# State-space scan and attention kernel: late bfloat16 splits, normalization on ScalarE, a third open convolution, first loads reordered

## The chip, the cores and the metric

The kernel runs on one core of one Trainium2 chip. The metric is device time in microseconds of one execution. Eight executions took 10527.92 to 10549.25 us, median 10539.07. The engines are TensorE (PE, its weight loads PEld), VectorE (DVE), ScalarE (ACT), GpSimd (POOL) and SyncE (SP), whose queue issues nearly all DMAs.

## What is computed

The input `x` is 8 images of 64 x 64 tokens of 96 channels. Layer 0 is a state-space block, layer 1 an attention without softmax and a feed-forward with 8-bit products:

```python
x = x + conv_ref(group_norm(x))                   # layer 0
t = tokens(x)
t = t + attn_ref(layer_norm(t))                   # layer 1
t = t + ffn_ref(layer_norm(t))
# conv_ref:
xin, z = split(einsum(x, in_proj_w))              # 192 channels each
xc = silu(depthwise_conv_3x3(xin) + conv_b)
xs = [row-wise, column-wise, and both reversed]   # K = 4 directions
dts, Bs, Cs = split(einsum(xs, x_proj_weight))    # 6, 16, 16 rows
delta = softplus(dts @ dt_projs_weight + bias)
h = h * exp(delta * A) + (delta * u) * B          # 4096 steps, 16 states
y = sum over n of h * C, + D * u                  # the four directions added
out = (layer_norm(y) * silu(z)) @ out_proj_w
```

## The kernel before

Three passes follow each other: `pass1` (L233), the projections and convolutions of all batches; `pass2` (L517), the scans; `pass3` (L823), everything after. Memory pools are opened per pass. What one pass hands to the next goes through DRAM.

**Order of work.** Each kind of work is a Python generator that names the engine and an assumed cost before each of its instructions, or a key that must be done. `weave` (L140) lets at most `room[kind]` units of a kind be open, and picks again and again the unit whose step can start earliest by these costs, the lower rank winning a tie. `InOrder` (L81) keeps the instructions of each engine in the order in which they were picked. So every engine, SP's queue too, works strictly in order, and a waiting instruction holds all behind it. The helper `issue` (L88, L89) records nearly all instructions, which is why the profile has L89 almost everywhere.

**Pass 1**, by pairs of batches. The 192 channels of two batches are cut in three chunks of 128: the first 128 channels of either batch, and the last 64 of both.
- `statistics` (L305) loads 512 tokens (`xs`), transposes them on PE into one of two PSUM buffers `pt`, and takes `bn_stats` on DVE. `group_norm` (L320) makes mean and inverse deviation `gm` of a batch; its power runs as two tiny POOL operations.
- `projection` (L348), eight units a batch, loads and transposes the tokens again (`xt`, `pt`), normalizes them to `xn` on DVE as (x - mean) times inverse deviation, multiplies by the weights on PE (`pa`, three products), and lets ACT copy to the padded image `xpad` and make SiLU of `z`. A batch's projections need the convolution that used its `xpad` before.
- `convolution` (L397) runs nine taps over 4096 elements on DVE into `u`, then SiLU and a transposed copy `ut` on ACT, and stores. Its taps wait for the taps of the convolution before it; the chunks go in the order 0, 2, 1.
- `x_projection` (L445), 16 units a batch, multiplies `u` on PE (`px`, three PSUM buffers) and copies the result to `xd` (ACT; every second one on DVE in the last batch; three buffers), which is stored to `xd_d`.
- `split` (L473), six units a batch, makes three bfloat16 parts of the rows for B and for delta, whose sum is the float32 value: it loads `bq` from `xd_d`; ACT casts it to part 0; a subtraction leaves the rest in `bq`; ACT casts part 1; a second subtraction gives part 2; two DMAs store `bs` to `b_d` or `dt_d`. The subtractions are POOL's, and DVE's in the last batch.

**Pass 2** takes 192 pieces: 4 pairs x 3 channel chunks x 4 directions x 4 pieces of 1024 steps; chunks 0 and 1 are full (one batch on 128 partitions), chunk 2 is split between two batches. `prepare` (L548) loads `xdt` (six DMAs), then `xb` and `u`, and makes B transposed (`bT`), `delta`, `du` = delta * u and its transpose `duT`. For each of 16 states n, `decay` (L619) makes `da` = exp(delta * A) on ACT, `products` (L657) brings du * B into a PSUM buffer `wide` (three of them) by one of three ways (`WAYS`: ACT's `x`, POOL's `xg`, or DVE's product), and `scan` (L681) runs the recurrence on DVE into `h`. For each two states, `load_c` (L607) loads C spread over the partitions (`c`, 1 MB, six buffers), `times_c` (L720) multiplies by `h` on POOL, and `sum_over_n` (L734) adds into `acc` on PE. The `xb` and `xdt` of a piece are the splits of its two batches; C is read from `xd_d` in float32.

**Pass 3** is not touched.

Of the kernel before, what the change touches and what calls it, by code (L numbers as in the profile page):

```python
# [33 lines left out]
F32 = mybir.dt.float32  # L34
# [8 lines left out]
P = 128  # L43
# [10 lines left out]

WAYS = [([2, 4, 6, 8, 10, 12, 14, 15], [3, 9]), ([3, 5, 7, 10, 13, 15], [2, 6, 12])]
NS = 3
GRP = 512
NG = L // GRP
RPG = GRP // WW
# [169 lines left out]
    return a_neg, dsum, dt_b, dt_w, sel, sel2  # L229


@with_exitstack
def pass1(ctx, tc, g, consts, ident, mhalf, engines, u_d, z_d, xd_d, b_d, dt_d):  # L233
    nc = tc.nc
# [85 lines left out]
    def group_norm(b):  # L320

        yield "st", b
        yield "dve", 0.2
        mv = two.tile([C, 2], F32, name="mv")
        dve.bn_aggr(mv, sts[b].rearrange("p a b -> p (a b)"))
        yield "pe", 0.3, 0.3, mms
        pm, slot = ps_mm.tile([P, GRP], F32, name="pm", tag="mm"), mms.taken
        pe.matmul(pm[0:C, 0:1], gmat, mv[:, 0:1], start=True, stop=True)
        end = yield "dve", 0.5
        mms.release(slot, end)  # L330
        gm = wp.tile([C, 2], F32, name=f"gm{b}")
        dve.tensor_copy(gm[:, 0:1], pm[0:C, 0:1])
        dq = two.tile([C, 1], F32, name="dq")
        dve.tensor_sub(dq, mv[:, 0:1], gm[:, 0:1])
        dve.scalar_tensor_tensor(dq, dq, dq, mv[:, 1:2], ALU.mult, ALU.add)
        yield "pe", 0.3, 0.3, mms
        pv, slot = ps_mm.tile([P, GRP], F32, name="pv", tag="mm"), mms.taken
        pe.matmul(pv[0:C, 0:1], gmat, dq, start=True, stop=True)
        end = yield "dve", 0.2
        mms.release(slot, end)  # L340
        dve.tensor_copy(gm[:, 1:2], pv[0:C, 0:1])
        end = yield "pool", 1.0
        pool.tensor_scalar(gm[:, 1:2], gm[:, 1:2], 1e-5, None, ALU.add)
        pool.tensor_tensor(gm[:, 1:2], gm[:, 1:2], mhalf[0:C, 0:1], ALU.pow)
        gms[b] = gm
        done["stats", b] = end

    def projection(b, q):  # L348

        pair, j = b // 2, b % 2  # L350
        cols = slice(q * GRP, (q + 1) * GRP)
        rows = slice(1 + q * RPG, 1 + (q + 1) * RPG)
        inner = slice(1, WW + 1)
        own, other = slice(64 * j, 64 * j + 64), slice(64 - 64 * j, P - 64 * j)
        third = xpad[2 + pair % 2]
        yield "stats", b
        yield "sp", 0.6, 4.0
        x = transposed(four, "xt", b, q)
        next(x)
        if pair > 0:  # L360
            yield "conv", pair - 1, j
        if pair > 1:
            yield "conv", pair - 2, 2
        yield "pe", 0.7, 0.3, pts
        pt, slot = next(x), pts.taken
        end = yield "dve", 0.8
        pts.release(slot, end)
        xn = four.tile([C, GRP], F32, name="xn")
        dve.tensor_scalar(xn, pt[0:C, :], gms[b][:, 0:1], gms[b][:, 1:2], ALU.subtract, ALU.mult)
        def product(w):  # L370
            yield "pe", 0.75, 0.4, mms
            p = ps_mm.tile([P, GRP], F32, name="pa", tag="mm")
            pe.matmul(p, w, xn, start=True, stop=True)
            return p, mms.taken

        pa, slot = yield from product(w_in[:, 0:P])
        end = yield "act", 0.6
        act.copy(xpad[j][:, rows, inner], pa.rearrange("p (h w) -> p h w", w=WW))
        mms.release(slot, end)
        pa, slot = yield from product(w_mix[:, j, :])  # L380
        yield "act", 0.6
        act.copy(third[own, rows, inner], pa[own, :].rearrange("p (h w) -> p h w", w=WW))
        z1 = three.tile([P, GRP], F32, name="z1")
        end = yield "act", 0.6
        act.activation(z1[other, :], pa[other, :], AF.Silu)
        one_more(("proj", b), NG, end)
        mms.release(slot, end)
        pa, slot = yield from product(w_in[:, DI : DI + P])
        z0 = three.tile([P, GRP], F32, name="z0")
        end = yield "act", 0.6  # L390
        act.activation(z0, pa, AF.Silu)
        mms.release(slot, end)
        yield "sp", 0.9
        sp.dma_start(z_d[b][P:DI, cols], z1[other, :])
        sp.dma_start(z_d[b][0:P, cols], z0)
# [49 lines left out]
    def x_projection(b, o, q):  # L445
        pair, j = b // 2, b % 2
        yield "u", pair, j
        yield "u", pair, 2
        px = None
        for ty, u in ((0, us[pair, j]), (1 + j, us[pair, 2])):  # L450
            end = yield ("pe", 0.62, 0.4) if px else ("pe", 0.62, 0.4, pxs)
            if px is None:
                px, slot = ps_px.tile([P, GRP], F32, name="px", tag="px"), pxs.taken
            if o == 0:
                src = u[:, q * GRP : (q + 1) * GRP]
            else:

                src = u.rearrange("p (h w) -> p h w", w=WW)[:, :, q * RPG : (q + 1) * RPG]
            pe.matmul(px, w_xp[:, ty, o, :], src, start=ty == 0, stop=ty > 0)
        one_more(("xproj", b), 2 * NG, end)  # L460
        by_dve = b == NB - 1 and q % 2 == 1
        end = yield ("dve" if by_dve else "act"), 0.6 if o == 0 else 0.8
        xd = three.tile([2 * NXD, GRP], F32, name="xd")
        src, dst = px[0 : 2 * NXD, :], xd
        if o == 1:
            src, dst = src.rearrange("p (h w) -> p w h", w=RPG), xd.rearrange("p (w h) -> p w h", w=RPG)
        (dve.tensor_copy if by_dve else act.copy)(dst, src)
        pxs.release(slot, end)
        end = yield "sp", 0.9, 3.0
        sp.dma_start(xd_d[b][o][:, q * GRP : (q + 1) * GRP], xd)  # L470
        one_more(("xd", b, o), NG, end)

    def split(b, o, row, rows, pieces, at, dst):  # L473

        wide, used = GRP, rows * pieces
        name, cost, by = ("dve", 0.65, dve) if b == NB - 1 else ("pool", 4.4 if b < NB - 2 else 2.5, pool)
        yield "xd", b, o
        yield "sp", 0.7, 4.0
        bq = three.tile([P, wide], F32, name="bq")
        src = xd_d[b][o][row : row + rows].rearrange("r (s t) -> (r s) t", s=pieces)  # L480
        sp.dma_start(bq[0:used], src[:, at : at + wide])
        yield "act", 0.6
        bs = three.tile([P, NS, wide], BF16, name="bs")
        act.copy(bs[0:used, 0, :], bq[0:used])
        yield name, cost
        by.tensor_sub(bq[0:used], bq[0:used], bs[0:used, 0, :])
        yield "act", 0.6
        act.copy(bs[0:used, 1, :], bq[0:used])
        yield name, cost
        by.tensor_sub(bs[0:used, 2, :], bq[0:used], bs[0:used, 1, :])  # L490
        yield "sp", 0.9
        half = used // 2
        for k2 in range(2):
            to = dst[k2].rearrange("e n (s t) -> (n s) e t", s=pieces)[:, :, at : at + wide]
            sp.dma_start(to, bs[half * k2 : half * (k2 + 1)])

    units = []
    for pair in range(NB // 2):
# [7 lines left out]
        for b in batches:  # L506
            for o in range(2):
                units += [("xproj", x_projection(b, o, q)) for q in range(NG)]
                units += [("split", split(b, o, 0, 2 * N, 4, at, b_d[b][o])) for at in (0, GRP)]
                units.append(("split", split(b, o, DT0, 2 * R, 8, 0, dt_d[b][o])))  # L510
    later_loads()
    room = {"proj": 4, "norm": 1, "stats": 3, "xproj": 3, "split": 3, "conv": 2}
    weave([(kind, (list(room).index(kind), i), unit) for i, (kind, unit) in enumerate(units)], room, done)


# [1 line left out]
def pass2(ctx, tc, g, ident, engines, fixed, u_d, xd_d, b_d, dt_d, y_d):  # L517
# [22 lines left out]
    def one_more(key, of, end):  # L540
        counts[key] = counts.get(key, 0) + 1
        if counts[key] == of:
            done[key] = end
# [4 lines left out]
    def prepare(at):  # L548
# [4 lines left out]
        parts = chunk_rows(pair, c)  # L553
        if at > 1:
            yield "scans", at - 2
        yield "sp", 2.5, 3.0
        xdt = one.tile([2 * NS * NS * R, T], BF16, name="xdt")
        for j in range(2):
            for m in range(NS):
                row = (j * NS + m) * NS * R  # L560
                sp.dma_start(xdt[row : row + NS * R, :], dt_d[2 * pair + j][o][k2].rearrange("s r t -> (s r) t")[:, cols])
        yield "sp", 1.5, 3.0
        xb = two.tile([KB, T], BF16, name="xb")
        for j in range(2):
            sp.dma_start(xb[j * NS * N : (j + 1) * NS * N, :], b_d[2 * pair + j][o][k2].rearrange("s n t -> (s n) t")[:, cols])
# [37 lines left out]
        act.copy(made[at][4], pt)  # L603
        slots["wide"].release(slot, end)
        done["duT", at] = end

    def load_c(at, m):  # L607
        pair, c, k, pc = pieces[at]
# [187 lines left out]
    for at, (pair, c, k, pc) in enumerate(pieces):  # L796
# [19 lines left out]
                add("term", 0, times_c(at, n // 2), n)  # L816
                add("sum", -4, sum_over_n(at, n // 2), n)
        add("acc", 0, take_acc(at), N)
    weave(units, {"prep": 1, "c": 1, "da": 2, "x": 1, "xg": 1, "dbu": 2, "scan": 2, "carry": 1, "term": 1, "sum": 1, "acc": 1}, done)


@with_exitstack
# [283 lines left out]
```

## Time and profile before

| what | value |
|---|---|
| median of 8 runs | 10539.07 us |
| profiled execution, its own time | 10533.8 us |
| its span | 10532.0 us |
| busy: DVE / ACT / POOL / PE | 9636.3 / 9296.5 / 9255.2 / 7582.7 us |
| mean granted TensorE clock | 0.901 |
| first tap of the first convolution | 72.6 us |
| end of the last tap of the last convolution | 701.3 us |
| first decay `da` of the scan pass | 807.3 us |

A line of a timeline gives start, duration, engine, line, operation, output and inputs, and in brackets how long the engine had been idle and what ended that. A line of a group gives the shape and the count, then busy time and mean nanoseconds of one, then the idle time just ahead of its instructions and what ended most of it. A line of the stage windows gives for each engine the busy time and the number of instructions, then the granted clock, the busy share of the DMA engines and what they moved. `SPq` is SP's queue. Neighbouring records of one engine overlap by some hundredths of a microsecond.

### The profile page before, as it was taken

The page shows a single profiled execution, that of the slowest core. Times are in us where ns is not written, and L with a number is a line of the kernel's source. Part 1 is how long each engine was busy: PE and PEld are TensorE (multiplying, and loading weights), DVE is VectorE, ACT ScalarE, POOL GpSimd, SP SyncE. Part 2 cuts the span into 40 slices and gives each one's busy share as a digit, 9 for nine tenths or more (in the row PEclk, how much of TensorE's full clock was granted, in tenths as well). Part 3 has the DMA queues.
Part 4 walks back from the last instruction along what each step waited for, and adds up shares of the span by engine and source line. Part 5 has one row for each costly group of instructions (what it writes and reads, how often), then busy time and mean ns, then how long its engine had stood idle before and what let it go on. Part 6 is the DMA issues. An engine that isn't in the chain of part 4 may idle for free.

```text
span 10532.0 us, 151336 instructions
## 1 busy us (share of the span) xinstructions
PE 7582.7 (72%) x51232; PEld 6175.8 (59%) x51232; DVE 9636.3 (91%) x6986; ACT 9296.5 (88%) x21363; POOL 9255.2 (88%) x3259
## 2 busy tenths in 40 slices
PE   6756777777677777777677777777777777776887
PEld 3325666566556566665565666655566666655665
DVE  7868999999999999999999999999999999997776
ACT  4649999999999999999999999999999999996665
POOL 2548999999999999999999999999999999997886
PEclk8878999998999999989999999988999999997776
DMA  5766666678976666699966666899766667997442
GB/s 155 231 199 201 203 221 212 218 206 199 203 216 209 217 218 209 214 200 200 215 209 217 214 213 214 202 202 200 218 210 216 218 203 217 201 200 177 123 130 60
DMA packets 928008, 2103.21 MB, mean 200 GB/s; under 512 B 274391, under 2 KB 422648, under 8 KB 925700
## 3 DMA queue, kind: packets, MB, share of 16 engines
q1 hardware_dynamic: 919812, 2092.79, 69.9%
q8 instruction: 410, 6.72, 0.3%
q14 instruction: 362, 2.97, 0.1%
q10 hardware_dynamic: 7424, 0.74, 0.1%
HBM read 1917.59 MB, written 175.66 MB: 199 GB/s over the span
## 4 chain that ended last, share of the span: by engine, by line
ACT 28%; DVE 22%; issue 17%; PE 16%; POOL 12%; DMA 4%; SPq 1%; DVEq 0%; POOLq 0%; ACTq 0%
DVE h L89 15%; ACT x L89 13%; ACT da L89 10%; POOL c L89 8%; PE wide L89 6%; PE acc L89 6%; DVE wide L89 4%; PE mm L89 2%; DMA xd_d<-xd 1%; ACT L89 1%; DVE u L89 1%; PE pa L89 1%; DMA xdt<-dt_d 1%; POOL xg L89 1%; ACT delta L89 1%
## 5 line engine op out<-in xcount | busy, mean ns | idle before, releaser
L89 POOL TENSOR_TENSOR c<-c,h 128x2048 f32<-128x2048 f32 x1536 | 6967.3, 4550 | 396.8 <-DVE h L89 336.4
L89 DVE TENSOR_TENSOR_SCAN h<-da,carry,wide 128x1024 f32<-128x1024 f32 x2304 | 5253.1, 2330 | 206.5 <-PE wide L89 137.7
L89 ACT ACTIVATE x<-duT,bT 128x128 f32<-128x128 f32 (+1 forms) x14336 | 4154.9, 366 | 57.1 <-PE wide L89 51.2
L89 PE MATMUL acc<-ident,c 128*128 128x128 f32 x24576 | 3472.1, 297 | 554.2 <-POOL c L89 546.0
L89 ACT ACTIVATE da<-delta,a_neg 128x1024 f32<-128x1024 f32 x3072 | 3504.0, 1144 | 346.4 <-DVE h L89 335.1
L89 PEld LDWEIGHTS acc<-ident,c 128*128 128x128 f32 x24576 | 3125.1, 155 | 886.8 <-POOL c L89 753.0
L89 PE MATMUL wide<-ident,x 128*128 128x128 f32 x11264 | 1605.5, 290 | 866.1 <-DVE h L89 845.0
L89 PEld LDWEIGHTS wide<-ident,x 128*128 128x128 f32 x11264 | 1336.5, 149 | 1162.1 <-DVE h L89 512.5
L89 DVE TENSOR_TENSOR_SCAN h<-da,wide 128x1024 f32<-128x1024 f32 x768 | 1707.7, 2270 | 84.9 <-PE wide L89 61.1
L89 DVE TENSOR_TENSOR wide<-du,wide 128x1024 f32<-128x1024 f32 x1216 | 1458.7, 1211 | 142.1 <-PE wide L89 141.9
L89 PE MATMUL wide<-xb,sel 96*128 96x512 bf16 x2432 | 751.8, 394 | 598.3 <-DVE h L89 505.8
L89 POOL TENSOR_TENSOR xg<-duT,bT 128x512 f32<-128x512 f32 (+1 forms) x640 | 892.3, 1410 | 78.0 <-PE wide L89 58.1
L89 PEld LDWEIGHTS <-sel 96*128 96x128 bf16 x2432 | 222.3, 101 | 789.0 <-DVE h L89 392.8
L89 PE MATMUL wide<-ident,xg 128*128 128x128 f32 x3584 | 498.4, 284 | 246.6 <-DVE h L89 240.2
L89 PEld LDWEIGHTS wide<-ident,xg 128*128 128x128 f32 x3584 | 410.0, 146 | 323.7 <-issue 155.9
L89 POOL TENSOR_TENSOR du<-delta,u 128x1024 f32<-128x1024 f32 x192 | 455.2, 2371 | 139.4 <-ACT delta L89 129.7
L89 ACT ACT_TABLE_LOAD x385 | 494.0, 1283 | 6.8
L89 DVE SCALAR_TENSOR_TENSOR u<-xpad,conv_w,u 128x4096 f32<-128x4096 f32 x96 | 452.7, 4716 | 1.2
L89 PE MATMUL px<-u,w_xp 128*128 128x512 f32 x512 | 260.0, 647 | 105.2 <-ACT u L89 65.1
L89 PE MATMUL mm<-w_out,gt 128*128 128x96 f32 (+1 forms) x1024 | 267.3, 381 | 40.2 <-POOL gt L89 21.8
L89 PEld LDWEIGHTS mm<-w_out,gt 128*128 128x128 f32 (+1 forms) x1024 | 204.2, 246 | 105.4 <-issue 36.3
L89 PE MATMUL wide<-ident,du 128*128 128x128 f32 x1536 | 210.4, 282 | 61.9 <-DVE h L89 44.5
(133 smaller groups left out, 5877.6 us busy)
## 6 DMA issues: line engine op xcount, KB each, us to landing
c<-xd_d SPq DMA_DIRECT2D x1024, 1024.0 KB
c<-xd_d SPq DMA_DIRECT2D x1024, 512.0 KB
u<-u_d SPq DMA_DIRECT2D x128, 512.0 KB
xdt<-dt_d SPq DMA_DIRECT2D x1152, 36.0 KB
xb<-b_d SPq DMA_DIRECT2D x384, 96.0 KB
u<-u_d SPq DMA_DIRECT2D x128, 256.0 KB
y_d<-y SPq DMA_DIRECT2D x24, 1024.0 KB
y<-y_d SPq DMA_DIRECT2D x64, 384.0 KB
```

What stands on the lines that cost most here:

```text
L89: ins = getattr(self.engine, op)(*args, **kwargs).ins
```

## The change

1. `split` leaves `pass1`, becomes a function of its own, and always subtracts on POOL, at an assumed cost of 4.4. Batches 0 to 4 are still split in pass 1, two splits open at a time instead of three. The 18 splits of batches 5, 6 and 7 (`LATE = 5`) are made in pass 2, one at a time, with buffers of their own; split i gets the rank of piece 5 (i + 1). `prepare` waits for the splits of its late batches.
2. `xn` is made by ACT as scale * x + bias straight from PSUM; `group_norm` gets one more small DVE operation, which waits for POOL's power, for the bias.
3. Three convolutions may be open instead of two, and four x-projections instead of three with four `xd` buffers instead of three.
4. In the first piece of pass 2, the loads of `xb` and `u` are picked together with those of `xdt`, so that fewer C loads stand ahead of them in SP's queue.

```diff
+LATE = 5
+def split(engines, pool_of, src, row, rows, pieces, at, dst):
+    act, pool, sp = engines
+    wide, used = GRP, rows * pieces
+    yield "sp", 0.7, 4.0
+    bq = pool_of.tile([P, wide], F32, name="bq")
+    src = src[row : row + rows].rearrange("r (s t) -> (r s) t", s=pieces)
+    sp.dma_start(bq[0:used], src[:, at : at + wide])
+    yield "act", 0.6
+    bs = pool_of.tile([P, NS, wide], BF16, name="bs")
+    act.copy(bs[0:used, 0, :], bq[0:used])
+    yield "pool", 4.4
+    pool.tensor_sub(bq[0:used], bq[0:used], bs[0:used, 0, :])
+    yield "act", 0.6
+    act.copy(bs[0:used, 1, :], bq[0:used])
+    yield "pool", 4.4
+    pool.tensor_sub(bs[0:used, 2, :], bq[0:used], bs[0:used, 1, :])
+    yield "sp", 0.9
+    half = used // 2
+    for k2 in range(2):
+        to = dst[k2].rearrange("e n (s t) -> (n s) e t", s=pieces)[:, :, at : at + wide]
+        sp.dma_start(to, bs[half * k2 : half * (k2 + 1)])
+def splits(b, o, b_d, dt_d):
+    return [(0, 2 * N, 4, at, b_d[b][o]) for at in (0, GRP)] + [(DT0, 2 * R, 8, 0, dt_d[b][o])]
...
-        end = yield "pool", 1.0
+        yield "pool", 1.0
         pool.tensor_scalar(gm[:, 1:2], gm[:, 1:2], 1e-5, None, ALU.add)
         pool.tensor_tensor(gm[:, 1:2], gm[:, 1:2], mhalf[0:C, 0:1], ALU.pow)
+        end = yield "dve", 0.2
+        dve.scalar_tensor_tensor(gm[:, 0:1], gm[:, 0:1], -1.0, gm[:, 1:2], ALU.mult, ALU.mult)
...
-        end = yield "dve", 0.8
+        end = yield "act", 0.6
         pts.release(slot, end)
         xn = four.tile([C, GRP], F32, name="xn")
-        dve.tensor_scalar(xn, pt[0:C, :], gms[b][:, 0:1], gms[b][:, 1:2], ALU.subtract, ALU.mult)
+        act.activation(xn, pt[0:C, :], AF.Identity, bias=gms[b][:, 0:1], scale=gms[b][:, 1:2])
...
-        xd = three.tile([2 * NXD, GRP], F32, name="xd")
+        xd = four.tile([2 * NXD, GRP], F32, name="xd")
...
-                units += [("split", split(b, o, 0, 2 * N, 4, at, b_d[b][o])) for at in (0, GRP)]
-                units.append(("split", split(b, o, DT0, 2 * R, 8, 0, dt_d[b][o])))
+                if b < LATE:
+                    units += [("split", after(("xd", b, o), split((act, pool, sp), two, xd_d[b][o], *w))) for w in splits(b, o, b_d, dt_d)]
-    room = {"proj": 4, "norm": 1, "stats": 3, "xproj": 3, "split": 3, "conv": 2}
+    room = {"proj": 4, "norm": 1, "stats": 3, "xproj": 4, "split": 2, "conv": 3}
...
+        for b in (2 * pair, 2 * pair + 1):
+            if b >= LATE:
+                yield "split", b
         yield "sp", 2.5, 3.0
         xdt = one.tile([2 * NS * NS * R, T], BF16, name="xdt")
...
-        yield "sp", 1.5, 3.0
+        if at > 0:
+            yield "sp", 1.5, 3.0
         xb = two.tile([KB, T], BF16, name="xb")
...
+    def late_split(b, o, which):
+        yield from split((act, pool, sp), one, xd_d[b][o], *which)
+        one_more(("split", b), 6, 0.0)
...
-    weave(units, {"prep": 1, "c": 1, "da": 2, "x": 1, "xg": 1, "dbu": 2, "scan": 2, "carry": 1, "term": 1, "sum": 1, "acc": 1}, done)
+    last = [(b, o, w) for b in range(LATE, NB) for o in range(2) for w in splits(b, o, b_d, dt_d)]
+    units += [("split", 5 * N * (i + 1), late_split(*which)) for i, which in enumerate(last)]
+    weave(units, {"prep": 1, "c": 1, "da": 2, "x": 1, "xg": 1, "dbu": 2, "scan": 2, "carry": 1, "term": 1, "sum": 1, "acc": 1, "split": 1}, done)
```

## The prediction

> **What bounds the kernel now.** I read the stage windows first. The scan pass runs from about 810 to 9600 us and is 83% of the span; the change touches the pass before it, the hand-over, and the first quarter of the scan pass.
>
> Windows of the convolution stretch (72 to 702), of the hand-over (702 to 812), and of two scan stretches (full and split channel chunks):
>
> ```profile
> core 0: us, PE busy (x) PEld busy (x) DVE busy (x) ACT busy (x) POOL busy (x), PEclk, DMA share, GB/s
> 72.00:702.00 630.00, 453.31 (x1230) 208.41 (x1228) 557.70 (x242) 353.79 (x477) 298.67 (x84) 0.86 0.67 203
> 702.00:812.00 110.00, 35.39 (x89) 15.40 (x90) 13.94 (x21) 39.60 (x50) 16.04 (x13) 0.66 0.66 210
> 860.00:1560.00 700.00, 505.08 (x3706) 429.44 (x3705) 670.19 (x349) 654.96 (x1427) 652.36 (x171) 0.93 0.65 212
> 2320.00:2980.00 660.00, 463.90 (x3251) 393.70 (x3249) 617.90 (x326) 641.57 (x1724) 617.30 (x208) 0.90 0.91 201
> ```
>
> DVE paces the convolutions (89% busy, 72.3 us idle). In the hand-over nothing is busy: a chain of waits. In the scans DVE leads (95.7%), with POOL (93.2%) and ACT (93.6%) close behind; in the split chunks ACT leads (97.2%).
>
> DVE's groups in 72 to 702 say what a removal is worth:
>
> ```profile
> L89 DVE SCALAR_TENSOR_TENSOR u<-xpad,conv_w,u 128x4096 f32<-128x4096 f32 x96 | 452.7, 4716 | 1.2
> L89 DVE TENSOR_SCALAR xn<-pt,gm 96x512 f32<-96x512 f32 x56 | 43.9, 801 | 32.4 <-PE pt L89 30.7 <-POOL bs L89 1.0 <-POOL gm L89 0.5
> L89 DVE BATCH_NORM_STATS2 st<-pt 96x6 f32<-96x512 f32 x48 | 32.1, 684 | 24.5 <-PE pt L89 24.4
> L89 DVE TENSOR_SCALAR u<-xpad,conv_w 128x4096 f32<-128x4096 f32 x12 | 29.8, 2484 | 13.3 <-ACT xpad L89 13.3
> ```
>
> The timelines of DVE, ACT, SP and POOL show the hand-over and the price of a subtraction:
>
> ```profile
> 696.84 4.48 DVE L89 SCALAR_TENSOR_TENSOR u<-xpad,conv_w,u 128x4096 f32<-128x4096 f32 x1
> ...
> 811.39 2.36 DVE L89 TENSOR_TENSOR wide<-du,wide 128x1024 f32<-128x1024 f32 x2 [31.77 <-PE wide L89]
> ```
>
> ```profile
> 705.43 0.58 ACT L89 COPY xd<-px 76x512 f32<-76x512 f32 x1 [10.86 <-DMA xd_d<-xd]
> ...
> 715.87 1.14 ACT L89 CAST bs<-bq 96x512 bf16<-96x512 f32 x2 [3.11 <-DMA bq<-xd_d]
> 716.92 3.89 ACT L89 ACTIVATE u<-u,conv_b 128x2048 f32<-128x2048 f32 x2
> ...
> 807.29 3.23 ACT L89 ACTIVATE da<-delta,a_neg 128x1024 f32<-128x1024 f32 x3
> ```
>
> ```profile
> 784.35 5.41 SPq L89 DMA_DIRECT2D c<-xd_d  x4
> 789.80 1.34 SPq L89 DMA_DIRECT2D xb<-b_d  x2
> ```
>
> ```profile
> 647.74 10.62 POOL L89 TENSOR_TENSOR bs<-bq,bs 128x512 bf16<-128x512 f32 x2
> ...
> 710.96 2.26 POOL L89 TENSOR_TENSOR bq<-bq,bs 128x512 f32<-128x512 f32 x2 [18.44 <-ACT bs L89]
> ```
>
> The last tap ends at 701.3, the last SiLU starts only at 716.9 behind copies and casts that wait for DMAs, and the first decay `da` starts at 807.3. A subtraction is 5.3 us beside convolution taps and 1.15 us without them.
>
> **Part 1, the convolution stretch.** The built order keeps taps and statistics on DVE and puts each `xn` on ACT.
> - Off DVE: 56 `xn`. Neighbours overlap by about 0.08, so 0.72 each: 40 us.
> - Off the taps' path: batch 5's 12 of the 72 subtractions in this stretch. A tap with POOL idle is 4.46, the mean 4.716: 96 x 0.256 = 25 us for 72, 0.34 each, so 4 us. The Trainium skill, "SBUF — State Buffer", section "Who interferes with whom", has a vector operation with two SBUF inputs and a GpSimd operation that reads SBUF take turns for a whole instruction, which would be up to 12 x 1.15 = 14 us; the tap row, stretched by less, decides.
> - Idle: the 32.4 us ahead of `xn` go from DVE. What is late next is the projection chain itself: a first tap still needs eight projections, whose waits now show at the first tap (13.3 us now) or the statistics (24.5). I take 26 of the 32 as gained, nearest to the row, since ACT in this stretch is 56% busy.
> - Added on ACT: 64 `xn`. Copies from PSUM of 512 elements are 0.587, the gated activation with scale and bias (`gt<-tr`) 0.774; the latter has the same form: 49 us on an engine with 276 us idle here, cost nothing while it has that cover.
> - Added on DVE: one tiny multiply per batch (0.2 us) that waits for POOL's power. The two POOL operations take 0.2 and 0.6 alone (at 37 us) and 5 and 5.9 beside taps (at 126). Behind it queue the taps. DVE waiting frees POOL, so I take 1.5 x 6 = 9 us, between 0.8 and 6 each.
> - Fourth `xd` buffer, fourth open x-projection: ACT waited 118.6 us for `xd` stores here; SP waited 56.2 us for POOL's `bs`. Both serve the chain above, no term of their own. A third open convolution adds no DVE work; the taps already run in sequence.
>
> Sum: 40 + 4 + 26 - 9 = 61 gained, the last tap at about 640. Bounds: PE is 453 us of 630, 72%; if the projection chain keeps it to 75%, the stretch is 604, 26 gained. If all 32 us ahead of `xn` and half of the other 40 idle go, and the new wait is 1 us, 40 + 4 + 52 - 6 = 90.
>
> **Part 2, the hand-over.** Before, from the last tap to `da`: 15.6 to the SiLU, 36 for batch 7's 16 x-projections, 19 to the first C load (at 772.0; the splits of batches 6 and 7 are issued here), 35 of loads: 106. After, in the built order of the queues:
> - Batches 6 and 7's splits are gone from ACT, SP, POOL and DVE. The SiLU still follows batch 6's `xd` copies and batch 4's last casts: I take 3, between 0 and 15.6.
> - The x-projections are the same: 36. The 19 us go, since the first C load stands just ahead of the last `xd` store.
> - Loads: the first piece's `xb` and `u` now stand behind two C loads in place of six. But SP then issues the other four and the first split's `bq`, and ACT has that split's cast between `delta` and `da`. So `da` waits for `bq` behind all six: 6 x 1 MB + 1 MB more at the 250 GB/s that 5 MB took here from 781 to 803, 28 us, and 2 for the table load; 30, against 35. Without that cast it would be about 18.
>
> 106 - (3 + 36 + 30) = 37 gained; bounds 19 (SiLU as late, loads as long) and 52.
>
> **Part 3, 18 splits in the scan pass.** In the built order they spread over the first 48 or so of 192 pieces, the two subtractions of one split 10 to 50 POOL instructions apart; after that the order is the same. `prepare`'s new wait first bites at piece 96, some 40 pieces later: nothing.
> - POOL: 36 subtractions. `xg` of 128x512 runs at 1.07 in the scans and a `bq` subtraction without taps at 1.15: 41 us. POOL waits mostly for DVE's `h` (80 of 136 us idle up to 3000).
> - ACT: 36 casts x 0.617 = 22 us, about 6 us of it in split chunks, where ACT leads.
> - SP: 54 DMAs, 18 x (0.6 + 2 x 0.6) = 32 us of issuing, and stores that wait for POOL; C loads queue behind. SP itself waits 1547 us of 2140 for a free C slot, so this is covered while C is six deep.
>
> Nothing in the trace shows how much of 41 + 22 reaches DVE. It is 0 if the idle of POOL and ACT takes it, 63 if all is paid. With engines at 93 to 96% I take about half of POOL's and ACT's share in the split chunks: 25.
>
> **Sum.** -61 - 37 + 25 = -73 against the profiled execution's 10533.8 us: 10461. That execution is 5.3 under the median of the eight runs, so 10466 as a median. This kernel's measurement can't tell less than 0.2% (21 us) from no change.
>
> **Rivals.**
> - *The projections hold the convolutions.* The idle time only moves from `xn` to first taps: PE stays at 75%, 26 gained, the hand-over gives 25, the splits cost 25: -26, 10513. For it: PE's waits for `xd` (36.6 us) and SiLU (43.9). Against: from 400 to 450 PE ran 47.5 of 50. Chance 0.14; half of this case is within 0.2%.
> - *Splits paid in full:* -61 - 37 + 63 = -35, 10504. For it, three engines above 93%. Chance 0.08.
> - *Splits free, convolutions tight:* -90 - 52 = -142, 10397. Chance 0.16.
> - *Slower: ACT stands at the casts.* A split's first cast waits in order for `bq`, queued behind C loads, with `da` and `x` behind it. The `xb` load behind four C loads took 13 us (789.8 to 802.9). If 9 us reach DVE for each of 18: 162 - 73 = +89, 10628. It turns slower from 73 / 18 = 4.1 us each. Against: in steady scans C loads go one by one as slots free up, about 5 us apart, and before scans ACT idles (75.6 us ahead of `da` up to 3000). Chance 0.06.
>
> **How the numbers follow.** The forecast has 0.56, its own range 10440 to 10495. 10400 to 10522 leaves out the slower case, half of the free one and part of the first rival, about 0.18. Faster: 0.56 + 0.16 + 0.08 + half of 0.14, 0.87; same 0.07; slower 0.06.
>
> **What would show it.** Last tap near 640; no `xn` on DVE, ACT's at 0.77; `da` 65 to 72 us after the last tap with ACT idle ahead of the first cast for `bq`; subtractions in the scans at 1.15; the scan pass from first `da` to its last scan longer by 10 to 40 us, all before about 3000; the rest as before. I am wrong if the last tap stays past 675, or if ACT shows long waits for `bq` all along the first quarter of the scans.

## The result, and the profile after

| | before | after |
|---|---|---|
| median of the runs | 10536.73 us (28 runs) | 10571.16 us (10 runs, 10559.66 to 10588.51) |
| ratio, 95% interval | | 1.0035 [1.0026, 1.0043] |
| span of the profiled execution | 10532.0 us | 10580.4 us |
| first tap / last tap ends | 72.6 / 701.3 | 80.3 / 670.9 |
| first decay `da` / first scan | 807.3 / 813.7 | 760.6 / 761.8 |
| first scan to last scan | 8805.5 | 8903.7 |
| last scan to the end of the span | 912.8 | 914.9 |

The change makes the kernel slower by 0.35%, where I forecast 0.7% faster. The table, read from the two traces, already says where. The first scan starts 51.9 us earlier, so the passes that the change was aimed at did gain. From the first scan to the last it then loses 98.2. The two profiled executions differ by 48.4 us, the medians by 34.4: single executions of the changed kernel lie up to 17 us from their median.

Windows of the changed kernel, the convolution stretch and the hand-over (us, then busy time and count of PE, its weight loads, DVE, ACT, POOL, then granted clock, DMA share, GB/s):

```profile
80.30:670.90 590.60, 442.15 (x1219) 207.39 (x1218) 525.29 (x192) 383.46 (x517) 253.58 (x72) 0.86 0.68 206
670.90:760.60 89.70, 37.78 (x93) 16.07 (x91) 7.87 (x11) 22.86 (x23) 4.52 (x3) 0.74 0.65 203
```

The convolution stretch is 590.6 long in place of 628.8 (the window of before, of 630.0, is a little wider) and starts 7.7 later; the hand-over is 89.7 in place of 106. DVE's idle time in the first is 65.3, against 72.3 before: it hardly fell.

The same 1200 us of the scan pass, before the change and after it:

```profile
1000.00:2200.00 1200.00, 861.16 (x6357) 730.85 (x6358) 1150.38 (x599) 1125.28 (x2447) 1123.50 (x293) 0.94 0.65 213
```

```profile
1000.00:2200.00 1200.00, 869.05 (x6184) 764.15 (x6185) 1124.72 (x582) 1100.60 (x2385) 1108.57 (x301) 0.89 0.65 210
```

This is the line that does not fit the prediction. If the splits' work on POOL and ACT held the scans up, those engines would be busier than before. Both are idler (POOL 1108.57 against 1123.50, though it now subtracts as well; ACT 1100.60 against 1125.28), DVE is 25.7 us idler and does 17 instructions fewer. These three wait more. PE alone is busier, with fewer matmuls, at a granted clock of 0.89 in place of 0.94.

To see when the loss comes, I take the start of each piece's `du` on POOL, counted from the first `du`, and subtract the same for before:

| piece | 4 | 8 | 12 | 20 | 32 | 40 | 48 | 60 | 100 | 190 |
|---|---|---|---|---|---|---|---|---|---|---|
| after is late by, us | 10.9 | 11.3 | 17.8 | 31.4 | 47.9 | 76.9 | 83.6 | 106.1 | 106.6 | 106.3 |

The first 11 are there from the first pieces on. Some 8 of them are no loss of the scans: after the change the first `du` stands 15.8 us ahead of the first scan, before it 7.6, since `da` then waits at the first split's cast (in the two runs below where that cast does not stand between `delta` and `da`, the lag of the first pieces is 0 to 4). From piece 8 to 60 the lag grows, unevenly, by 95. The last late split ends in piece 59, and from piece 60 on the lag stays at about 106. So the cost lasts as long as splits are open. Their own instructions are short, as groups of POOL show from 760 to 3300:

```profile
L91 POOL TENSOR_TENSOR c<-c,h 128x2048 f32<-128x2048 f32 x429 | 1947.9, 4551 | 160.2 <-DVE h L91 141.3 <-PE acc L91 8.9 <-ACT x L91 3.2
L91 POOL TENSOR_TENSOR bq<-bq,bs 128x512 f32<-128x512 f32 x12 | 14.0, 1168 | 11.1 <-ACT bs L91 11.1
L91 POOL TENSOR_TENSOR bs<-bq,bs 128x512 bf16<-128x512 f32 x11 | 12.9, 1172 | 0.0
```

A subtraction takes 1.17 us, as predicted, and only one of them was waited for on an idle POOL (11.1 us, the first split's). The casts' waits for `bq` in all 36 casts come to 28.1 us, 12.8 of it in the hand-over. Neither makes 98.

**Theory.** The planner assumes 4.4 us for a late subtraction. With that cost it picks another order for everything else while splits are open, and the order itself is slow. **Rival:** the splits' execution (42 us of POOL, 22 of ACT, 54 DMAs) holds the scans up.

### The profile page after: what moved, and what is told of

Same layout as the page of the kernel before. It is cut to its first block, busy times and chain, and to the rows that moved or that the text cites. A ratio compares the mean times of both kernels' runs of the same rounds, so it can differ in the third digit from the quotient of the medians.

```text
span 10580.4 us, 151226 instructions
## 1 busy us (share of the span) xinstructions
PE 7656.5 (72%) x51232; PEld 6293.9 (59%) x51232; DVE 9595.1 (91%) x6918; ACT 9344.0 (88%) x21427; POOL 9239.3 (87%) x3271
## 4 chain that ended last, share of the span: by engine, by line
ACT 29%; DVE 23%; issue 17%; PE 17%; POOL 11%; DMA 3%; SPq 1%; DVEq 0%; ACTq 0%; POOLq 0%
DVE h L91 16%; ACT x L91 13%; ACT da L91 10%; POOL c L91 7%; PE acc L91 6%; PE wide L91 6%; DVE wide L91 3%; PE mm L91 2%; ACT L91 1%; DMA xd_d<-xd 1%; DVE u L91 1%; POOL xg L91 1%; ACT delta L91 1%; DMA xdt<-dt_d 1%; PE px L91 1%
## 5 line engine op out<-in xcount | busy, mean ns | idle before, releaser
L91 PE MATMUL acc<-ident,c 128*128 128x128 f32 x24576 | 3509.3, 300 | 477.9 <-POOL c L91 445.6
L91 PEld LDWEIGHTS acc<-ident,c 128*128 128x128 f32 x24576 | 3185.8, 157 | 787.1 <-POOL c L91 617.1
L91 PE MATMUL wide<-ident,x 128*128 128x128 f32 x11264 | 1631.2, 293 | 852.9 <-DVE h L91 827.8
L91 PEld LDWEIGHTS wide<-ident,x 128*128 128x128 f32 x11264 | 1361.3, 150 | 1148.4 <-DVE h L91 495.2
L91 PE MATMUL wide<-ident,xg 128*128 128x128 f32 x3584 | 526.7, 295 | 284.9 <-DVE h L91 276.2
L91 PEld LDWEIGHTS wide<-ident,xg 128*128 128x128 f32 x3584 | 437.0, 152 | 360.6 <-issue 205.7
```

Of the source, the lines that this page charges most:

```text
L91: ins = getattr(self.engine, op)(*args, **kwargs).ins
```

## Experiments on the scan pass: order or execution

### The order kept, the work taken away

Every engine keeps the instructions of the changed kernel in the same order, with one more that clears `bs` ahead of them. The late splits work on 16 of 512 columns: in the first run the subtractions and casts, in the second the subtractions alone. The lines for the first:

```diff
-def split(engines, pool_of, src, row, rows, pieces, at, dst):
+def split(engines, pool_of, src, row, rows, pieces, at, dst, w=GRP, bs=None):
...
-    act.copy(bs[0:used, 0, :], bq[0:used])
+    act.copy(bs[0:used, 0, 0:w], bq[0:used, 0:w])
...
-    pool.tensor_sub(bq[0:used], bq[0:used], bs[0:used, 0, :])
+    pool.tensor_sub(bq[0:used, 0:w], bq[0:used, 0:w], bs[0:used, 0, 0:w])
...
-    act.copy(bs[0:used, 1, :], bq[0:used])
+    act.copy(bs[0:used, 1, 0:w], bq[0:used, 0:w])
...
-    pool.tensor_sub(bs[0:used, 2, :], bq[0:used], bs[0:used, 1, :])
+    pool.tensor_sub(bs[0:used, 2, 0:w], bq[0:used, 0:w], bs[0:used, 1, 0:w])
...
+    bs_late = one.tile([P, NS, GRP], BF16, name="bs")
+    pool.memset(bs_late, 0.0)
...
-        yield from split((act, pool, sp), one, xd_d[b][o], *which)
+        yield from split((act, pool, sp), one, xd_d[b][o], *which, w=16, bs=bs_late)
```

> The changed kernel with the same order of instructions on every engine, but the two casts and two subtractions of each of the 18 late splits work on 16 of 512 columns (batches 5 to 7 thus get wrong parts; DMAs are unchanged). The scan pass, from the first da to the last scan, took 8811.9 us before and 8904.8 us with the change, +92.9. Theory ORDER (the planner's assumed 4.4 us for each subtraction rearranged the queues of PE, ACT, DVE and POOL, and the rearranged order is slower by itself): +70 to +93 stays, the kernel near 10550 to 10570. Theory EXECUTION (the 41 us of subtractions and 22 us of casts, doubled by coupling of three nearly full engines): +0 to +15, near 10480 to 10495.

> As the one before, but the casts are whole and only the subtractions of the late splits are cut to 16 columns. ORDER: +70 to +93 in the scan pass. EXECUTION by POOL: +10 to +30; EXECUTION by ACT's casts: +50 to +80.

Measured, one run each: 10554.04 us with both tiny, 10570.62 with the subtractions tiny, against 10538.04 for before and 10571.16 for after. First scan to last scan: 8896.6 and 8899.1, against 8903.7 after and 8805.5 before (from the first `da`, as the expectation counts, 85.9 and 88.4 more than before). The window of the first run, almost without the splits' arithmetic:

```profile
1000.00:2200.00 1200.00, 866.54 (x6161) 760.15 (x6162) 1124.80 (x581) 1094.49 (x2383) 1093.52 (x300) 0.89 0.67 211
```

DVE is as idle as in the changed kernel, and the clock is as low. Taking the arithmetic away returns 7.1 of the 98.2 us, less than profiles with one and the same order of the scans differ among themselves (8809 to 8819 below). So the arithmetic of the splits is not what costs. Their loads and stores run in full here; the next test has them too.

### The work kept, the order of before

The late splits keep all their work. Their planned costs are zero; the waits that the planner assumes between their steps stay as long as they were. They are over sooner, in piece 18 and not 59.

```diff
-def split(engines, pool_of, src, row, rows, pieces, at, dst):
+def split(engines, pool_of, src, row, rows, pieces, at, dst, plan=(0.7, 4.0, 0.6, 0.3, 4.4, 0.3, 0.9)):
...
-    yield "pool", 4.4
+    yield "pool", plan[4], plan[5]
...
-        yield from split((act, pool, sp), one, xd_d[b][o], *which)
+        yield from split((act, pool, sp), one, xd_d[b][o], *which, plan=(0.0, 4.7, 0.0, 0.9, 0.0, 4.7, 0.0))
```

> The changed kernel, all work done, but the late splits have an assumed cost of zero in the plan (their delays are kept), so that in the scan pass all other instructions of PE, DVE, ACT and POOL stand in the order of the kernel before, but for a swap of 16 PE and 4 ACT instructions far behind. ORDER: the scan pass +0 to +25, the kernel 10490 to 10515. EXECUTION: +80 to +100, near 10570.

Measured: 10475.67 us over 4 runs, ratio to before 0.9940 [0.9925, 0.9955]. The time is below the expected 10490 to 10515, the scan pass is as expected: first scan to last scan is 8809.3, within 4 us of before. (These are single profiles. Four more versions below with late splits planned like this took 8811 to 8819, the three kernels with before's order and no late splits 8794 to 8806. By the means the work itself costs some 14 us.) Its window has before's clock and nearly before's counts on every engine, with the splits' work on POOL besides (1147.82 busy):

```profile
1000.00:2200.00 1200.00, 857.50 (x6352) 721.95 (x6351) 1148.02 (x598) 1130.53 (x2462) 1147.82 (x319) 0.94 0.68 218
```

The two tests agree from either side: with the slow order and hardly any arithmetic it is slow, with all the work, the DMAs too, and the old order it is fast.

### What the planned cost does to the order

The next run tells the planner about the truth, 1.2 us a subtraction, and leaves its other costs.

```diff
-        yield from split((act, pool, sp), one, xd_d[b][o], *which)
+        yield from split((act, pool, sp), one, xd_d[b][o], *which, plan=(0.7, 4.0, 0.6, 0.3, 1.2, 0.3, 0.9))
```

> The changed kernel with one number different: the planner is told 1.2 us for a late subtraction, about what one takes in the scans (1.16 to 1.18 measured), in place of 4.4. All other planned costs of a late split stay. Theory A (the planner's error is what costs: told a true duration, it finds as good an order as before): the scan pass, first decay to last scan, takes 8810 to 8825 us as in the run with no planned cost, the time is 10475 to 10490. Theory B (any planned occupation of the engines changes the order, and the order of before is a fine balance which a truth does not keep): the scan pass stays 30 us or more above 8810, the time is over 10505; pieces 0 to 60 take over 2770 us, against 2727 before, 2746 with no planned cost and 2833 with 4.4.

Measured: 10500.93 us over 5 runs, ratio 0.9967 [0.9954, 0.9980]. I leave the late splits' own instructions out of the lists and count, from the start of the scan pass to the end of the kernel, the positions at which another operation or other tiles stand than before. They and the time from the first scan to the 961st (60 pieces of 16) go together:

| planned cost of a subtraction, us | 0 | 1.2 | 4.4 |
|---|---|---|---|
| positions of 54048 on PE that differ | 16 | 1308 | 6132 |
| of 6678 on DVE | 0 | 52 | 260 |
| of 20817 on ACT | 4 | 795 | 2053 |
| of 3138 on POOL | 0 | 56 | 261 |
| 960 scans, us (before 2739.0) | 2750.5 | 2767.3 | 2837.6 |

(At zero, the splits' other planned costs are zero too.) Neither theory of this run holds as I put it (from the first `da` the scan pass takes 8834.0). The time is between the two bounds: the truth costs much less than the error, but it is not free. It is the whole truthful plan that is priced here, the planned casts and DMAs too, not the 1.2 us alone. The lag against before grows only up to piece 20, where the splits end, and stays at 32 to 37 us from there: the shorter planned splits are over sooner. So the loss is made while splits are open, at a rate set by how far the plan is disturbed.

The last run of this group asks whether the splits are needed for it at all. It is the kernel before with one number changed, the assumed duration of the C product (4.55 by the profile):

```diff
-        end = yield "pool", 4.55, 0.2
+        end = yield "pool", 4.96, 0.2
```

> The kernel before, no instruction added or removed; only the cost that the planner assumes for the product with C on POOL is 4.96 us in place of 4.55 (it takes 4.55): 0.41 more per product is what the 18 late splits' assumed 158 us came to per product of the 48 pieces they lie in. Theory ORDER (an assumed overload of POOL alone makes the planner stand the queues in an order that costs some 2 us a piece): slower by 100 to 350 us, 10640 to 10890. If the lost time needs the splits themselves (their loads, their buffers, their instructions): within 20 us of before.

Measured, one run: 10725.74 us, against 10537.42; first scan to last scan 8986.8, 181.3 more than before. No instruction was added; only the order differs. This kernel's order is a fine balance, and an assumed cost that is off by 0.4 us upsets it.

### How the other order is slow

Around one `prepare` in the changed kernel PE's timeline reads:

```profile
1094.63 1.04 PE L91 MATMUL acc<-ident,c 128*128 128x128 f32 x8
1095.88 0.34 PE L91 MATMUL wide<-sel,xb 96*128 96x16 bf16 x8 [0.21 <-DVE h L91]
1099.46 0.60 PE L91 MATMUL wide<-xdt,dt_w 108*128 108x512 bf16 x2 [3.23 <-DVE h L91]
1099.90 3.24 PE L91 MATMUL acc<-ident,c 128*128 128x128 f32 x16
1102.93 1.43 PE L91 MATMUL wide<-ident,xg 128*128 128x128 f32 x8
```

and DVE's in the same time:

```profile
1095.74 1.21 DVE L91 TENSOR_TENSOR wide<-du,wide 128x1024 f32<-128x1024 f32 x1
1097.05 4.58 DVE L91 TENSOR_TENSOR_SCAN h<-da,carry,wide 128x1024 f32<-128x1024 f32 x2
1104.46 2.35 DVE L91 TENSOR_TENSOR_SCAN h<-da,carry,wide 128x1024 f32<-128x1024 f32 x1 [2.82 <-PE wide L91]
```

Before, at the like place:

```profile
1147.20 0.34 PE L89 MATMUL wide<-sel,xb 96*128 96x16 bf16 x8 [1.00 <-DVE h L89]
1148.73 1.29 PE L89 MATMUL acc<-ident,c 128*128 128x128 f32 x8 [1.19 <-POOL c L89]
1149.82 1.06 PE L89 MATMUL wide<-xdt,dt_w 108*128 108x512 bf16 x2
1150.67 1.91 PE L89 MATMUL acc<-ident,c 128*128 128x128 f32 x8
1152.38 1.30 PE L89 MATMUL wide<-ident,xg 128*128 128x128 f32 x8
```

Both products of `prepare` (`sel,xb` and `xdt,dt_w`) need one of the three `wide` buffers, which a scan has to release. Before, eight sums into `acc` stand between the two and use the time of that release. After, the two follow each other directly: PE stands 3.23 us for the scan, then has sixteen sums to do at once, and the `wide` that DVE wants next is behind them. DVE stands 2.82. This is one place of many, but it recurs. PE's idle time ahead of the `xdt` product from 1335 to 2235, in the order before, after, after's order without the work, before's order with the work:

```profile
L89 PE MATMUL wide<-xdt,dt_w 108*128 108x512 bf16 x40 | 14.3, 446 | 0.3 <-DVE h L89 0.2
```

```profile
L91 PE MATMUL wide<-xdt,dt_w 108*128 108x512 bf16 x40 | 15.2, 470 | 33.0 <-DVE h L91 33.0
```

```profile
L91 PE MATMUL wide<-xdt,dt_w 108*128 108x512 bf16 x38 | 14.3, 465 | 29.8 <-DVE h L91 29.8
```

```profile
L91 PE MATMUL wide<-xdt,dt_w 108*128 108x512 bf16 x40 | 14.5, 450 | 0.5 <-DVE h L91 0.5
```

The wait goes with the order, not with the work. But it is not time that PE waits in addition. PE's waits in the same stretch, before and after:

```profile
PE wide L89 <- DVE h L89: 196.4, 185, 2.9
PE acc L89 <- POOL c L89: 46.7, 65, 2.0
```

```profile
PE wide L91 <- DVE h L91: 218.5, 157, 3.2
PE acc L91 <- POOL c L91: 10.5, 10, 1.7
```

(A line gives who waited for whom, then us in total, times, the longest.) In all PE waits 253 times for 247.5 us before and 180 times for 249.5 us after: as long, but less often and longer at a time. DVE, which leads in the scans, then waits more for PE:

```profile
DVE h L89 <- PE wide L89: 23.6, 17, 2.1
```

```profile
DVE h L91 <- PE wide L91: 40.3, 21, 3.8
```

The same wait is 38.3 us in after's order without the work and 24.8 in before's order with it; DVE's whole idle time in these 900 us is 32.8 before, 56.5 after, then 54.6 and 34.8. The lag grows by 30 in this stretch. Which of the moved pairs makes how much of the 95 us was not shown: no run moves them one by one.

## Experiments on the parts of pass 1 and the hand-over

These start from the version with zero planned costs (10475.67 us, "the base"), so that the scan pass does not blur them.

### All splits in pass 1

```diff
-LATE = 5
+LATE = NB
```

> The changed kernel with all splits in the first pass (by POOL, two open), so that the scan pass has the order and work of before; the other three parts of the change stay. Both theories: the scan pass +0 to +2. The first da, at 807.3 before and 760.6 with the change, tells what the late splits give the first pass: if they give most of the 46.7 us, it comes at 785 to 805; if the other parts do, at 762 to 780.

Measured: 10511.30 us over 7 runs, ratio 0.9973 [0.9962, 0.9985] (the planned costs do not matter here, since no split is late). The last tap ends at 671.0 as in the changed kernel, but the first scan follows 144.3 us later, against 90.9 with late splits and 112.3 before. The first `da` comes at 809.0, outside both ranges of the expectation: without the late splits the other parts bring nothing at `da`, although the last tap is 30 us earlier. So splitting late takes 53 us out of this hand-over (21 against that of the kernel before, where three splits may be open and batch 7's subtractions are DVE's); of the 53, 36 reach the end in the base, and with the changed kernel's order they turn into a loss of 60 (10571.16 against 10511.30).

### The first split not ahead of the first decay

In the changed kernel ACT's timeline has the first split's cast between `delta` and `da`, as predicted:

```profile
687.93 0.58 ACT L91 COPY xd<-px 76x512 f32<-76x512 f32 x1 [10.94 <-DMA xd_d<-xd]
688.41 3.89 ACT L91 ACTIVATE u<-u,conv_b 128x2048 f32<-128x2048 f32 x2
...
744.78 1.12 ACT L91 ACTIVATE delta<-wide,dt_b 128x1024 f32<-128x1024 f32 x1
758.67 0.62 ACT L91 CAST bs<-bq 128x512 bf16<-128x512 f32 x1 [12.77 <-DMA bq<-xd_d]
...
760.60 3.22 ACT L91 ACTIVATE da<-delta,a_neg 128x1024 f32<-128x1024 f32 x3
```

The run lets the late splits start when the second piece's scans are planned:

```diff
+        yield "scans", 1
         yield from split((act, pool, sp), one, xd_d[b][o], *which, plan=(0.0, 4.7, 0.0, 0.9, 0.0, 4.7, 0.0))
```

> As the run with assumed cost zero (10475.67 us, scan pass in before's order), and the late splits begin only when the scans of the second piece are done. In the changed kernel ACT stood 12.8 us at the first split's cast, waiting for bq, with delta made and the first da behind it. If that cast held the first da, da comes about 10 to 13 us earlier after the last x-projection (41 us there with the cast, 28 to 31 without) and the kernel is at 10460 to 10470. If something else holds da (C loads, table load), nothing changes: 10470 to 10482.

Measured: 10475.71 us over 5 runs, ratio 0.9937 [0.9924, 0.9951]. ACT's timeline:

```profile
742.39 1.11 ACT L91 ACTIVATE delta<-wide,dt_b 128x1024 f32<-128x1024 f32 x1
744.82 3.23 ACT L91 ACTIVATE da<-delta,a_neg 128x1024 f32<-128x1024 f32 x3
```

`da` follows `delta` after one table load, 26.9 us after the last x-projection in place of 41.4. But the first scan gains less, 33.2 in place of 42.6, and the medians are equal. Not to wait at that cast was worth 14 us at `da`, 9 at the first scan, and nothing that the times can tell; the 10460 to 10470 expected of it did not come.

### The first piece's loads

Part 4 undone in the base:

```diff
-        if at > 0:
-            yield "sp", 1.5, 3.0
+        yield "sp", 1.5, 3.0
```

> The version without planned costs of the late splits, with part 4 of the change undone: in the first piece the loads of xb and u are picked by themselves again. It prices part 4 alone. If the first loads matter as I reckoned in the hand-over (two C loads of 1 MB ahead of them in place of six, but the first split's cast holds the decay behind all six anyway): the first decay comes at most 5 us later and the time is 10475 to 10485. Rival: without it the first products wait for four more C loads, 16 us at 250 GB/s, the first decay near 770 in place of 756, the time near 10490.

Measured: 10483.38 us over 4 runs, ratio 0.9952 [0.9937, 0.9967]. From the last tap to the first scan it takes 94.0 us in place of 91.6. The rival's 16 us are not there: `da` stands behind the first split's cast either way, here with `delta` behind it too.

```profile
744.65 0.62 ACT L91 CAST bs<-bq 128x512 bf16<-128x512 f32 x1 [27.72 <-DMA bq<-xd_d]
...
747.68 1.12 ACT L91 ACTIVATE delta<-wide,dt_b 128x1024 f32<-128x1024 f32 x1
...
750.61 3.23 ACT L91 ACTIVATE da<-delta,a_neg 128x1024 f32<-128x1024 f32 x3
```

Whether part 4 is worth some microseconds or nothing, the intervals do not tell.

### Normalization and the third convolution, one without the other

First the normalization back on DVE in the base, with the extra multiply removed:

```diff
-        end = yield "act", 0.6
+        end = yield "dve", 0.8
...
-        act.activation(xn, pt[0:C, :], AF.Identity, bias=gms[b][:, 0:1], scale=gms[b][:, 1:2])
+        dve.tensor_scalar(xn, pt[0:C, :], gms[b][:, 0:1], gms[b][:, 1:2], ALU.subtract, ALU.mult)
```

> The run with assumed cost zero, with xn back on DVE as in the kernel before (and without the extra multiply). There the last tap ended at 665.5 us (671 to 674 and 662.5 in the other runs with the same first pass, 701.3 before). If xn on ACT gives the first pass its gain, the last tap goes to 690 to 705 and the kernel to 10495 to 10515; if the gain comes from the late splits, the fourth xd buffer and the third open convolution, it stays at 660 to 680 and 10470 to 10485.

Then, in the base, two open convolutions in place of three:

```diff
-    room = {"proj": 4, "norm": 1, "stats": 3, "xproj": 4, "split": 2, "conv": 3}
+    room = {"proj": 4, "norm": 1, "stats": 3, "xproj": 4, "split": 2, "conv": 2}
```

> The run with assumed cost zero, with two convolutions open in place of three. I expected nothing of the third: last tap 660 to 675, the kernel 10468 to 10485. If a third open convolution matters, the last tap is later by 10 us or more.

And the third open convolution alone in the kernel before:

```diff
-    room = {"proj": 4, "norm": 1, "stats": 3, "xproj": 3, "split": 3, "conv": 2}
+    room = {"proj": 4, "norm": 1, "stats": 3, "xproj": 3, "split": 3, "conv": 3}
```

> The kernel before with only the number of open convolutions changed from two to three; normalization stays on VectorE, all splits stay in pass 1. Theory A (the third open convolution pays by itself, since it lets the next batch's projections and statistics be issued ahead): the last tap comes 30 us or more earlier than 701.3, the time is 10480 to 10510. Theory B (it pays only together with the normalization on ScalarE, which loads the projections' chain differently): the last tap stays within 15 us of 701 and the time within 20 us of before.

Measured, first tap to end of the last tap, and time:

| | two open | three open |
|---|---|---|
| `xn` on DVE | 628.8 (before) | 630.6: 10536.13 us, ratio 1.0002 [0.9992, 1.0012] (kernel before); 638.9: 10518.53, 0.9980 [0.9971, 0.9989] (base) |
| `xn` on ACT | 655.2: 10540.73, 1.0006 [0.9997, 1.0015] (base) | 585.0: 10475.67, 0.9940 (base) |

(Profiles of one and the same pass 1 differ in this stretch by up to 12 us: 581.3 to 592.8 in seven of the changed order, 628.8 and 640.3 in two of before's.) With `xn` back on DVE the last tap is at 711.2, a little past the expected range; with two open it is at 734.9, far past the 660 to 675 that I expected; the third open convolution alone gives Theory B, 704.1. Neither part pays by itself: the third convolution alone does nothing, and `xn` on ACT with two open convolutions makes the stretch no shorter, rather longer. Together, with the other parts of the base, they take 44 us off (628.8 to 585.0). DVE's groups say why. With `xn` on ACT and two open:

```profile
L91 DVE SCALAR_TENSOR_TENSOR u<-xpad,conv_w,u 128x4096 f32<-128x4096 f32 x96 | 453.7, 4726 | 2.3
L91 DVE BATCH_NORM_STATS2 st<-pt 96x6 f32<-96x512 f32 x48 | 32.2, 688 | 100.9 <-PE pt L91 100.9
L91 DVE TENSOR_SCALAR u<-xpad,conv_w 128x4096 f32<-128x4096 f32 x12 | 29.9, 2490 | 35.0 <-ACT xpad L91 35.0
```

In the base the same groups idle 24.6 and 40.7. The difference is the statistics. DVE's timeline with two open convolutions, at the largest of these waits:

```profile
426.70 21.15 DVE L91 SCALAR_TENSOR_TENSOR u<-xpad,conv_w,u 128x4096 f32<-128x4096 f32 x4
481.87 0.70 DVE L91 BATCH_NORM_STATS2 st<-pt 96x6 f32<-96x512 f32 x1 [34.02 <-PE pt L91]
```

After the last tap that it has DVE's next instruction is a statistic of a later batch, and PE, which works on x-projections and projections all this time, comes to that batch's `pt` only 34 us later. With a third convolution open, its taps can be put there. With `xn` on DVE two were enough; I take it that DVE, with its 44 us more, had less time to fill, which no run shows by itself. So the slack that the move of `xn` made on DVE is only worth what else is ready to be put in it.

## Why the prediction was wrong, point by point

**Part 3, the 18 splits (+25, between 0 and 63): this step failed.** The sizes in it were right: 1.17 us a subtraction, casts of 0.61, and 7.1 us for the arithmetic with the order held, 11.5 for all of it over 960 scans where the order of before is kept (some 14 by the means of several profiles): less than the 25, within its bounds. I wrote that after the first 48 or so pieces the order is the same (it is from piece 60 on), and priced in the pieces before only what is executed. That the order of the other instructions differs there, on every engine, got no term. With the work it costs 98.6 us over 960 scans, of which 91.8 remain without the arithmetic. No rival had it either. My bounds came from busy times, and a busy time can't bound what a change of order does.

**The slower rival (ACT stands at the casts, 10628)** ended on the right side by the wrong mechanism. Its casts wait 28.1 us in all, 12.8 of it in the hand-over, and with the order of before the same casts wait 22.6 and the scans are within 4 us of before.

**Part 1, the convolutions (61, between 26 and 90): half the size, and its condition not seen.** The last tap came 30 us earlier, at 670.9 and not near 640. By terms:

- `xn` off DVE: its 43.9 us are gone, 40 net, as predicted. An `xn` on ACT takes 0.773, as predicted.
- Taps: 4 us gained were predicted for 12 subtractions fewer beside them. The taps rose from 4.716 to 4.763, 4 us lost. With the same 60 subtractions the mean was 4.645 with `xn` on DVE and 4.780 in the base, so the count of subtractions does not set it. What the taps lose by the taking of turns in the Trainium skill's "SBUF — State Buffer", section "Who interferes with whom", stays undecided here: it would have made 12 fewer subtractions worth up to 14 us, and other neighbours of the taps moved at the same time.
- Idle ahead of `xn` (26 of 32.4 gained): this is the term that was too large. Two thirds of it went to the first taps:

```profile
L91 DVE BATCH_NORM_STATS2 st<-pt 96x6 f32<-96x512 f32 x48 | 31.8, 684 | 25.8 <-PE pt L91 25.7
L91 DVE TENSOR_SCALAR u<-xpad,conv_w 128x4096 f32<-128x4096 f32 x12 | 28.9, 2409 | 46.0 <-ACT xpad L91 43.5 <-DMA xd_d<-xd 2.5
L91 DVE SCALAR_TENSOR_TENSOR gm<-gm 96x1 f32<-96x1 f32 x6 | 3.8, 629 | 4.6 <-POOL gm L91 4.6
```

  Of the 46.0, 13.35 lie ahead of the very first tap, outside the stretch; of before's 13.3, 2.39 do. Inside it is 32.7 against 10.9, so 22 of the 32 came back as waits for `xpad`, and about 9 were gained. This is the first rival (the projections hold the convolutions): I gave it 0.14, and its 26 for the whole stretch is nearer than my 61. Its PE share of 75% is what the window after shows (442.15 of 590.60).
- The new multiply on DVE: 4.6 waiting and 3.8 working, 8.4 against 9.
- The first tap: 80.3 in place of 72.6, as the eight projections that it needs now go through ACT (with `xn` back on DVE it is at 72.3). I had no term for these 8 us.

  Together: 40 - 4 + 9 - 8 - 8 = 29, against 30 measured.
- "A third open convolution adds no DVE work" is true and misled me: without it Part 1 gains nothing.

**Part 2, the hand-over (37, between 19 and 52): 16 gained, below my lower bound.** From the last tap to `da` it takes 89.7 us, not 69.

- The last SiLU came 17.5 after the last tap and not 3: it stands behind `xd` copies that wait for stores (10.94), and these, not the splits, set that time. My own lines showed the same wait before, 10.86.
- The x-projections took 32.3, against 36.
- From there to `da` it is 39.9, against 30. The first C load is issued 7.5 after the last x-projection; I had taken all 19 us up to it as gone.

```profile
728.17 0.39 SPq L91 DMA_DIRECT2D c<-xd_d  x1
```

  The loads from there on take 32.4, near the 30 (5 MB in 22 us are some 230 GB/s, not the 250 that I used).
- That ACT stands at the first split's cast was right (12.77, in the lines above), and so was that without it the loads let `da` go much sooner (26.9 after the last x-projection, 14 less). That this would be worth as much at the end was not.

**The sum.** With before's order kept, the three terms of the base are 35.8 for the last tap (665.5), 20.7 to the first scan and -3.8 over the scans, 53 us by the traces, and 62 by the medians. My 73 is near that by luck, two errors that partly cancel: 98 in place of 56 for parts 1 and 2, and 25 in place of 4 for part 3. As built, the order adds 94 and turns it into a loss. I had said that I would be wrong if the last tap stayed past 675, or if long waits for `bq` ran through the first quarter of the scans; neither was the case.

**The better version.** The changed kernel with the late splits at no planned cost takes 10475.67 us, 0.9940 of before, and beats both kernels. So most of the forecast gain was there, if by other terms; the order that the plan made took it back.

## What to carry to other kernels

Where queues are filled by a planner, a changed or added planned cost is a change to every instruction planned beside it, and it has to be priced as that: see how many positions differ and for how long, and test it by keeping the work and planning it at nothing, or keeping the order and taking the work away. A true cost is not a safe one: with 1.2 us in the plan for 1.17 on the chip, and the splits' casts and DMAs planned too, 25 of the 62 us were given back. Time freed on an engine is a gain only if other work is open to be put there, so a limit on open units and a move of work off the busy engine belong together and should be tried together.

## What the runs showed of the hardware

- The granted PE clock of the scans went with the order of the queues: 0.94 from 1000 to 2200 us before and in the base, 0.92 with 1.2 planned, 0.89 in the changed kernel and 0.89 in its order without the splits' arithmetic. With 1.2 planned it is 0.90 from 1000 to 1500, while the splits are open, and 0.93 from 1700 to 2200, after them (before: 0.93 and 0.94). From 1335 to 2235 the sums into `acc` took 293 ns before and 301 after, the products with `xg` 281 and 328. The Trainium skill's "TensorE: Matmul & The Clock Gate", Part 1, says that activity releases the throttle; here the lower clock is seen where PE waits longer at a time (1.39 us on average from 1335 to 2235 in place of 0.98), with about as much busy time (651.8 and 648.9 of 900). That the longer waits lower the clock no run shows by itself. How much of the loss is the clock and how much the waits, no run here separates.
- Pass 1 of the changed kernel, with the same instructions in the same order, ended its last tap anywhere from 662.5 to 673.6 us in seven profiles. A few microseconds of that stretch can't be read from single profiles.
- PE can be busier while it does less: 869.05 us for 6184 matmuls against 861.16 for 6357. PE's busy share alone would not have told which of the two kernels is the faster.
